# Spreading token scalars over a graph by VectorE and transfers instead of a matmul, with softmax, weight sums and seams moved, in a four-layer graph network

## The chip, the core and the metric

The kernel runs on one core of a Trainium2 chip. The core has five engines with a queue each, which work in order and meet through semaphores: TensorE (PE; its weight loads are listed as PEld), VectorE (DVE), ScalarE (ACT), GpSimd (POOL) and SyncE (SP), which here only issues transfers. The metric is the device time of one execution in microseconds (us), the median of several runs. All data are fp32.

## The reference

The input x has 128 graphs of 64 nodes with 512 features. Each layer adds to x what it computes from h = relu(layernorm(x)):

```python
# layer 0 (att over the 64 nodes i of a graph; mask is all ones)
agg = einsum('bij,bjd->bid', adj, h @ Wk)
w   = inv_scale * mask * einsum('bid,bid->bi', h @ Wq, agg)
x   = x + softmax(w, axis=1)[:, :, None] * (h @ Wv)
# layer 1
weight = adj * exp(einsum('bqd,bkd->bqk', query, keyt))
x   = x + (weight / weight.sum(2)) @ value
# layer 2: 8 heads, scores * (adj + adj), softmax, context, output product
# layer 3
sj = (h @ Wv + bv) @ aw[:512];  si = (h @ Wv + bv) @ aw[512:]
e  = leaky_relu(sj[:, None, :] + si[:, :, None] + ab, 0.2)
tr = adj * exp(e) / (sum + 1e-12)
x  = x + relu(h @ Wk0 + tr @ h @ Wk1 + tr @ tr @ h @ Wk2 + biases)
```

Two places need a scalar per token on every token of its graph: the softmax of layer 0 (the minimum and the sum of 64 values w) and the sums sj + si of layer 3.

## The kernel before

Tokens are worked in 32 blocks of 256 (four graphs, two tiles of 128 partitions, TT = 2, N = 64). Every 512x512 product of a block is a Strassen-like `Product`: seven products of quarters, whose operand sums S1 to S4 POOL makes (`sums`, L270 to L274) and whose parts are put together from two PSUM tiles `ab` and `dc` taken from a pool of four. `first` and `second` do the early matmuls and then keep copies: `keep_ab` copies on ACT (p1, L335) and adds on DVE (u2, L336), `keep_dc` copies on ACT (p5, L344 or L348). `late` does the rest on top of them, and `store` (L358 to L362), `store_T` (L366 to L382) or `add_to` write the result with ACT, DVE and POOL. Only when those have read a PSUM tile may a later product take it. `side_by_side` runs two products next to each other, with slots between their parts in which other work is issued (`between`).

`norm` (L185 to L217) takes the statistics on DVE (L185, L186, ve L188, mv L189), rstd and nmr on POOL (L191, L193), h on ACT (L200). ACT's queue writes h to DRAM in two pieces, SP's queue reads it back in four as `part`, and DVE turns it in 32x32 squares into the feature-major hT (L243).

Layers 0 and 1 are interleaved in steps (two blocks of layer 0, then two of layer 1, four steps a period); layer 2 is a loop over 32 blocks; layer 3 is a generator `layer3_step`: the head makes y2 and y1 (L306), the tail y0, the denominators (L966), po (L449), y (L977), then the dots hu (L915) of block b+2. Its end, two neighbour sums later, is tz on ACT (L1013), POOL (L1015) and DVE (L1016), issued from the head of the next step.

The program does not fix the order of an engine's queue alone. A scheduler places instructions by its own costs, and `tc.issue_after(i)` keeps what is issued under it behind instruction i. `behind`, `read`, `kept_ab` and `tail` are such marks. `chore` is one of the weight sums that POOL makes ahead of a later layer (L104).

A token scalar is spread over its graph by a product: DVE multiplies an eye by the scalar, which gives a diagonal block `wd` (L616) or `di` (L920), and `graph_sums` multiplies it by the block-diagonal matrix of ones (L457). In layer 0, `layer0_end` then takes the minimum (L627), the two exps on ACT (L633, L638), the weights att (L640, L641) and updates x (L643). In layer 3, `layer3_in` adds sj (L934), the leaky relu (L940), exp on ACT (L941) and the adjacency (L943).

Of the kernel before, what the change touches and what calls it, by code (L numbers as in the profile page):

```python
# [13 lines left out]
P = 128  # L14
# [12 lines left out]
def kernel(ctx: ExitStack, tc: tile.TileContext, a: dict, out: bass.AP):  # L27
# [72 lines left out]
    def chore(n: int = 1):  # L100
        with tc.issue_after(behind[0].ins):
            for _ in range(min(n, len(chores))):
                w, (to, x, y) = chores.pop(0)
                nc.gpsimd.tensor_tensor(w[:, to], w[:, x], w[:, y], ALU.subtract)  # L104
# [63 lines left out]
    eye = const.tile([P, N], FP, tag="eye", name="eye")  # L168
    for g in range(2):
        h = slice(g * N, (g + 1) * N)  # L170
        nc.vector.memset(ones_bd[h, h], 1.0)
        nc.vector.tensor_copy(eye[h, :], ident[h, h])
# [4 lines left out]
    behind_norm, parted = {}, {}  # L177
    read, w2 = [None], []

    def norm(x, name: str, home):  # L180
# [13 lines left out]
        behind_norm.setdefault(0, (by_rows, summed_up))  # L194
        h = med.tile([P, TT, D], FP, tag="h", name=f"h_{name}", bufs=homes["h"])
# [60 lines left out]
    behind = [None]  # L256
# [21 lines left out]
    class Product:  # L278
# [77 lines left out]
        def store(self, y):  # L356
# [4 lines left out]
            nc.vector.tensor_tensor(y[:, 0, F:], self.c, self.u2, ALU.add)  # L361
            nc.gpsimd.tensor_tensor(y[:, 1, F:], self.u3, self.p5, ALU.add)  # L362

        def store_T(self, y, bias):
# [8 lines left out]
            for m in range(2):  # L373
                f = slice(m * P, (m + 1) * P)
                self.taken = nc.vector.scalar_tensor_tensor(
# [78 lines left out]
    def graph_sums(e, cols: int, name: str):  # L454

        ps = ps_sc.tile([P, cols], FP, tag="sc", name=f"sm_{name}")
        nc.tensor.matmul(ps, ones_bd, e, start=True, stop=True)  # L457
        return ps

    def reciprocals(e, name: str):  # L460

        den = graph_sums(e.rearrange("p t i -> p (t i)"), TT * N, name)
        r = small.tile([P, TT, N], FP, tag="r", name=f"r_{name}", bufs=2)
        nc.vector.reciprocal(r.rearrange("p t i -> p (t i)"), den)
        return r
# [56 lines left out]
    def setup1():  # L522
# [43 lines left out]
        folded(kt, qt, 1, m, lambda: layer0_end(0, *softmax))  # L566
# [29 lines left out]
    def layer0(b: int, x, adjT, hs, hT, aggs, between):  # L596
# [10 lines left out]
        w = small.tile([P, TT], FP, tag="w", name=f"w_{b}")  # L607
        for t in range(TT):
            nc.vector.scalar_tensor_tensor(
# [3 lines left out]


        wd = small.tile([P, TT, N], FP, tag="e", name=f"wd_{b}")
        tail[0] = nc.vector.tensor_tensor(  # L616
            wd,
            eye.unsqueeze(1).to_broadcast([P, TT, N]),
            w.unsqueeze(2).to_broadcast([P, TT, N]),
            ALU.mult,  # L620
        )
        return x, gv, w, wd

    def layer0_end(b: int, x, gv, w, wd):
        wrow = graph_sums(wd.rearrange("p t i -> p (t i)"), TT * N, f"w_{b}")
        mn = small.tile([P, TT], FP, tag="mx0", name=f"mn0_{b}")
        nc.vector.tensor_reduce(  # L627
            mn, wrow.rearrange("p (t i) -> p t i", t=TT), AX.X, ALU.min
        )
        nc.vector.tensor_tensor(w, w, mn, ALU.subtract)  # L630
        tot = small.tile([P, TT], FP, tag="tot", name=f"tot_{b}")
        for t in range(TT):
            nc.scalar.activation(  # L633
                wd[:, t, :], wrow[:, t * N : (t + 1) * N], AF.Exp, bias=mn[:, t : t + 1],
# [272 lines left out]
    def layer3_dots(b: int, x, adjT, hs):  # L907
# [3 lines left out]
        sij = small.tile([P, 2, TT], FP, tag="sij", name=f"sij_{b}")  # L911
        for s in range(2):
            for t in range(TT):
                hu = med.tile([P, D], FP, tag="agg", name=f"hu_{b}_{s}_{t}", bufs=2)
                nc.vector.scalar_tensor_tensor(  # L915
                    hu, hs[t], 1.0, us[s], ALU.mult, ALU.mult,
                    accum_out=sij[:, s, t : t + 1],
                )
        di = small.tile([P, TT, N], FP, tag="e", name=f"di_{b}")
        nc.vector.tensor_tensor(  # L920
            di,
            eye.unsqueeze(1).to_broadcast([P, TT, N]),
            sij[:, 1, :].unsqueeze(2).to_broadcast([P, TT, N]),
            ALU.mult,
        )
        sj = small.tile([P, TT], FP, tag="sj", name=f"sj_{b}")
        nc.vector.tensor_scalar(sj, sij[:, 0, :], c3, None, ALU.add)
        return x, adjT, hs, di, sj

    def layer3_in(b: int, x, adjT, hs, e, sj, made: dict):  # L930


        pi = graph_sums(e.rearrange("p t i -> p (t i)"), TT * N, f"i_{b}")
        nc.vector.tensor_tensor(  # L934
            e,
            pi.rearrange("p (t i) -> p t i", t=TT),
# [180 lines left out]
    begun = []  # L1117
# [7 lines left out]
    for i, (layer, b) in enumerate(steps):  # L1125
        if i == n_steps - 4:
            fetch2(0)
        if i == n_steps - 3:
            fetch2(1)
        if i == n_steps - 1:  # L1130
            fetch2(2)
        between = [[], [lambda: chore(3 if i < 4 else 1)], []]
        if i == 1:
            begun = []
# [5 lines left out]
        for n, end in begun:  # L1140
            between[n].append(end)
        begun = []
# [10 lines left out]
        elif i + 2 == n_steps:  # L1153
            between[0].append(lambda: prepare2(0))
        else:
            between[0].append(lambda: prepare2(1))
        if layer == 0:
            softmax = layer0(b, *loaded[b], *normed[i], aggs.pop(b, None), between)
            begun = [(0, lambda b=b, softmax=softmax: layer0_end(b, *softmax))]
# [18 lines left out]
    w3, made_in, ops3 = {}, {}, {}  # L1178
# [4 lines left out]
    def layer3_step(b: int, ahead: bool = True):  # L1183
# [4 lines left out]
        x, al = made_in.pop(b)  # L1188
        ops = ops3.pop(b)
        coming = normed3  # L1190

        def begin():
# [3 lines left out]
            if b + 2 < n_blk and ahead:  # L1196
                with tc.issue_after(kept_ab[0].ins):
                    normed3 = layer3_norm(b + 2)

        def attention():  # L1200
            if b + 1 < n_blk:
                layer3_in(b + 1, *coming, made_in)

        y = layer3_head(b, ops, [[begin], [ending.pop()], [attention]])
        yield
# [8 lines left out]
        if b + 2 < n_blk:  # L1214
            with tc.issue_after(kept.ins):
                if ahead:
                    normed3 = layer3_dots(b + 2, *normed3)
                    fetch3(b + 3)
                else:
                    fetch3(b + 2)  # L1220
# [154 lines left out]
```

## Time and profile before

| | |
|---|---|
| three runs | 2524.32, 2524.8, 2526.9 us (median 2524.8) |
| profiled execution | 2527.1 us, its span 2524.5 us |
| mean granted clock of TensorE | 0.996 |
| PE busy | 2487.0 us in 19488 instructions |
| DVE busy | 1822.0 us in 4590 |
| POOL busy | 1324.1 us in 1710 |
| ACT busy | 857.1 us in 2106 |
| h to DRAM, issue to landing | 2.1 us (median of 252) |
| part from DRAM | 2.8 us (median of 504) |
| adjT from DRAM, 64 KB in 256-byte pieces | 2.2 us (median of 64) |
| c from c_row, one row to 128 partitions | 6.4 us (one) |

A busy time is the time in which an engine has an instruction in work; PE's matmuls are pipelined, so their durations overlap and the distance between two starts is what counts. In an order of time, a start to the next start is therefore often shorter than the duration beside it. "Idle before" names what ended the wait of an engine. A granted clock of 0.50 means that TensorE ran at half speed in that stretch.

### The profile page before, as it was taken

How to read it: one execution, taken by the hardware profiler on the slowest of the kernel's cores; microseconds unless marked ns; L12 is line 12 of the kernel's file. 1: busy time of each engine (PE TensorE's matmuls, PEld its weight loads, DVE VectorE, ACT ScalarE, POOL GpSimd, SP SyncE). 2: the span in 40 equal slices, each digit the busy share in tenths (PEclk: the TensorE clock that was granted, in tenths of full speed). 3: DMA queues.
4: the chain of work that ended last, by engine and by line, in shares of the span. 5: the costliest groups of instructions: out<-in, count | busy, mean ns of one | idle time of the engine just before them, and what ended most of it. 6: DMA issues, size and time to landing. Idle time of an engine off the chain costs nothing.

```text
span 2524.5 us, 52284 instructions
## 1 busy us (share of the span) xinstructions
PE 2487.0 (99%) x19488; PEld 2124.1 (84%) x19488; DVE 1822.0 (72%) x4590; ACT 857.1 (34%) x2106; POOL 1324.1 (52%) x1710
## 2 busy tenths in 40 slices
PE   9899999999999999999999999999989999999999
PEld 5788888888888888999999999999867777777776
DVE  5577777777777786667667667667568777777775
ACT  3333433333334332333333333333223333333332
POOL 2444343444433445666656556556465555555554
PEclk9999999999999999999999999999999999999999
DMA  7344343333343354443343343344433333333320
GB/s 180 94 127 124 111 127 114 119 107 116 113 126 112 122 156 138 128 133 108 122 132 115 123 131 115 122 136 134 139 112 104 104 103 107 105 106 106 103 77 34
DMA packets 305190, 295.50 MB, mean 117 GB/s; under 512 B 56870, under 2 KB 211494, under 8 KB 304936
## 3 DMA queue, kind: packets, MB, share of 16 engines
q1 hardware_dynamic: 258856, 208.26, 29.2%
q10 hardware_dynamic: 46080, 83.91, 9.1%
q8 instruction: 153, 2.51, 0.4%
q14 instruction: 101, 0.83, 0.1%
HBM read 158.91 MB, written 133.18 MB: 116 GB/s over the span
## 4 chain that ended last, share of the span: by engine, by line
PE 57%; DVE 2%; DMA 1%; POOL 1%; issue 1%; SPq 0%; ACT 0%; POOLq 0%; ACTq 0%; DVEq 0%
PE ab_y L306 13%; PE dc_y L306 9%; PE ab_v L306 4%; PE ab_q L299 4%; PE ab_k L299 4%; PE ab_o L306 4%; PE dc_q L299 3%; PE dc_k L299 3%; PE dc_v L306 3%; PE dc_o L306 3%; PE po L449 2%; PE pc L825 1%; PE s L750 1%; DVE hu L915 1%; DMA x<-x 0%
## 5 line engine op out<-in xcount | busy, mean ns | idle before, releaser
L200 ACT ACTIVATE h<-x,nmr,rstd 128x512 f32<-128x512 f32 x256 | 194.8, 806 | 207.6 <-POOL nmr L193 202.1
L270 POOL TENSOR_TENSOR S<-hT 128x256 f32<-128x256 f32 x128 | 97.8, 764 | 243.9 <-DVE hT L243 231.1
L306 PE MATMUL ab_y<-L_Wk,hT 128*128 128x256 f32 x768 | 204.9, 389 | 7.9 <-DVE u_y L336 6.7
L306 PE MATMUL ab_v<-L_Wv,hT 128*128 128x256 f32 x768 | 201.0, 384 | 3.7 <-DVE u_v L336 3.0
L306 PEld LDWEIGHTS ab_y<-L_Wk,hT 128*128 128x128 f32 x768 | 138.7, 190 | 74.9 <-DVE u_y L336 30.7
L191 POOL TENSOR_TENSOR rstd<-ve,neghalf 128x2 f32<-128x2 f32 x128 | 90.5, 707 | 209.2 <-DVE mv L189 190.7
L306 PE MATMUL dc_v<-L_Wv,S 128*128 128x256 f32 x768 | 198.0, 380 | 0.7 <-ACT p_v L344 0.7
L306 PE MATMUL ab_y<-L_Wk,S 128*128 128x256 f32 x768 | 198.0, 380 | 0.0
L306 PE MATMUL ab_v<-L_Wv,S 128*128 128x256 f32 x768 | 197.1, 379 | 0.0
L306 PE MATMUL dc_y<-L_Wk,S 128*128 128x256 f32 x768 | 193.5, 380 | 0.1
L243 DVE STREAM_TRANSPOSE hT<-part 128x512 f32<-128x512 f32 x252 | 174.4, 698 | 8.6 <-DMA part<-h_rows 5.9
L306 PEld LDWEIGHTS dc_y<-L_Wk,S 128*128 128x128 f32 x768 | 146.0, 191 | 21.3 <-issue 0.8
L306 PEld LDWEIGHTS ab_y<-L_Wk,S 128*128 128x128 f32 x768 | 146.5, 191 | 20.1
L185 DVE BATCH_NORM_STATS2 stats<-x 128x6 f32<-128x512 f32 x256 | 162.8, 677 | 0.0
L306 PEld LDWEIGHTS ab_v<-L_Wv,S 128*128 128x128 f32 x768 | 145.9, 190 | 19.8
L306 PEld LDWEIGHTS dc_v<-L_Wv,S 128*128 128x128 f32 x768 | 143.8, 191 | 20.0 <-ACT p_v L344 0.9
L306 PEld LDWEIGHTS ab_v<-L_Wv,hT 128*128 128x128 f32 x768 | 138.2, 190 | 21.9 <-DVE u_v L336 4.0
L915 DVE SCALAR_TENSOR_TENSOR hu<-h,us 128x512 f32<-128x512 f32 x128 | 139.4, 1139 | 1.9 <-POOL bs L894 1.4
L1015 POOL TENSOR_TENSOR tz<-tz,y 128x512 f32<-128x512 f32 x62 | 90.4, 1458 | 95.4 <-ACT tz L1013 95.3
L336 DVE TENSOR_TENSOR u_v<-ab_v,p_v 128x256 f32<-128x256 f32 x96 | 40.4, 421 | 126.4 <-ACT p_v L335 125.9
L1016 DVE SCALAR_TENSOR_TENSOR x<-tz,x 128x512 f32<-128x512 f32 x62 | 42.9, 692 | 112.3 <-POOL tz L1015 112.3
L272 POOL TENSOR_TENSOR S<-hT,S 128x256 f32<-128x256 f32 x128 | 113.0, 883 | 0.0
(257 smaller groups left out, 6181.7 us busy)
## 6 DMA issues: line engine op xcount, KB each, us to landing
x<-x SPq DMA_DIRECT2D x128, 512.0 KB, 3.8
h_rows<-h ACTq DMA_DIRECT2D x252, 256.0 KB, 2.1
part<-h_rows SPq DMA_DIRECT2D x504, 128.0 KB, 2.8
x<-in_x_dram SPq DMA_DIRECT2D x32, 512.0 KB, 3.7
e_rows<-et ACTq DMA_DIRECT2D x64, 256.0 KB, 3.0
pT<-e_rows SPq DMA_DIRECT2D x128, 128.0 KB, 3.1
out_dram<-x SPq DMA_DIRECT2D x31, 512.0 KB, 2.8
adjT<-in_adjT_dram SPq DMA_DIRECT2D x64, 64.0 KB, 2.2
```

The lines of the kernel that those rows point to most:

```text
L185: nc.vector.bn_stats(stats[:, t, :], x[:, t, :])
L191: nc.gpsimd.tensor_tensor(rstd, ve, neghalf, ALU.pow)
L200: nc.scalar.activation(hs[t], x[:, t, :], AF.Relu, bias=nmr[:, t : t + 1], scale=rstd[:, t : t + 1])
L243: nc.vector.transpose(hT[:, :, t * P : (t + 1) * P].rearrange("p k (g q) -> p g k q", q=Q), part[:, t * 4 : (t + 1) * 4].rearrange("p g (k ...
L270: nc.gpsimd.tensor_tensor(S1, A21, A22, ALU.add)
L272: nc.gpsimd.tensor_tensor(S4, A12, S2, ALU.subtract)
L299: nc.tensor.matmul(dst[:, m * P : (m + 1) * P], w[:, place, k, m * P : (m + 1) * P], left[:, k, :], start=key not in self.begun, stop=last ...
L306: nc.tensor.matmul(dst, left[:, k, :], w[:, place, k, :], start=key not in self.begun, stop=last and k == 1, skip_group_check=True,)
L449: nc.tensor.matmul(ps[t][half[g ^ t]], e[half[g], t, :], us[t][half[g]], start=True, stop=True)
L915: nc.vector.scalar_tensor_tensor(hu, hs[t], 1.0, us[s], ALU.mult, ALU.mult, accum_out=sij[:, s, t : t + 1],)
L1015: nc.gpsimd.tensor_tensor(tz[t], tz[t], y0[:, t, :], ALU.add)
L1016: nc.vector.scalar_tensor_tensor(x[:, t, :], tz[t], 0.0, x[:, t, :], ALU.max, ALU.add)
```

## The change

Token scalars no longer go through PE. They are written into the first two columns of a 128x32 tile that is zero elsewhere (`column_pair`, two of them in turn), DVE transposes its 32x32 squares into `lines`, SP writes the lines to a row in DRAM and reads it back twice, each time broadcast over the 64 partitions of a graph (`spread`). `graph_sums`, `eye`, `wd` and `di` as products are gone; 64 transposes, 128 row writes and 128 broadcast reads are added.

`layer0_end` of an even block (and of blocks 1 and 31) is issued in a new last slot of the next step, behind the DVE work of a store; that of the other odd blocks in the first slot of the step after the next, behind the norm's statistics. In layer 3, `layer3_in(b)` belongs to step b itself, norm(b+2) is placed behind the transfers of the last spread, and the load of x for b+3 behind the reads of h. POOL's weight sums are placed behind POOL's last store and behind nmr. At the seams the loads of layer 2 come earlier, its first norms behind the end of layer 0's step; the turn of e of block 31, the biases, loads, norms and dots of layer 3's first blocks are moved among the last three blocks of layer 2.

```diff
-    def chore(n: int = 1):
-        with tc.issue_after(behind[0].ins):
+    def chore(n: int = 1, also=()):
+        with ExitStack() as placed:
+            for i in (behind[0], *also):
+                placed.enter_context(tc.issue_after(i.ins))
...
-    def graph_sums(e, cols: int, name: str):
-
-        ps = ps_sc.tile([P, cols], FP, tag="sc", name=f"sm_{name}")
-        nc.tensor.matmul(ps, ones_bd, e, start=True, stop=True)
-        return ps
...
+    def spread(pair, name: str):
+
+        row = tc.dram_tile([TT, P], FP, name=f"{name}_row")
+        lines = small.tile([P, Q], FP, tag="lines", name=f"{name}_lines", bufs=2)
+        nc.vector.transpose(lines, pair)
+        for t in range(TT):
+            nc.sync.dma_start(
+                row[t : t + 1].rearrange("o (s q) -> (o s) q", q=Q), lines[t::Q]
+            )
+        to = small.tile([P, TT, N], FP, tag="e", name=name)
+        by_graph = row.rearrange("(o t) (g i) -> g o t i", o=1, g=2)
+        for g in range(2):
+            spread_out[0] = nc.sync.dma_start(
+                to[half[g]], by_graph[g].to_broadcast([N, TT, N])
+            )
+        return to
...
     def layer0_end(b: int, x, gv, w, wd):
-        wrow = graph_sums(wd.rearrange("p t i -> p (t i)"), TT * N, f"w_{b}")
...
-        nc.vector.tensor_reduce(
-            mn, wrow.rearrange("p (t i) -> p t i", t=TT), AX.X, ALU.min
-        )
+        nc.vector.tensor_reduce(mn, wd, AX.X, ALU.min)
...
-        between = [[], [lambda: chore(3 if i < 4 else 1)], []]
+        between = [[], [
+            lambda: chore(3 if i < 4 else 1, (stored[0], normalised[0]) if i else ())
+        ], [], []]
...
-            begun = [(0, lambda b=b, softmax=softmax: layer0_end(b, *softmax))]
+
+            late = b % 2 and 1 < b < n_blk - 1
+
+            def end0(b=b, softmax=softmax, late=late):
+                with tc.issue_after((counted[0] if late else stored[1]).ins):
+                    layer0_end(b, *softmax)
+
+            begun.setdefault(i + (2 if late else 1), []).append((0 if late else 2, end0))
...
             if b + 2 < n_blk and ahead:
-                with tc.issue_after(kept_ab[0].ins):
+                with tc.issue_after(kept_ab[0].ins), tc.issue_after(spread_out[0].ins):
                     normed3 = layer3_norm(b + 2)
 
         def attention():
-            if b + 1 < n_blk:
-                layer3_in(b + 1, *coming, made_in)
+            layer3_in(b, *dots3.pop(b), made_in)
...
                 if ahead:
-                    normed3 = layer3_dots(b + 2, *normed3)
-                    fetch3(b + 3)
+                    dots3[b + 2] = layer3_dots(b + 2, *normed3)
+                    with tc.issue_after(read[0].ins):
+                        fetch3(b + 3)
...
+        if b == n_blk - 2:
+            with tc.issue_after(read[0].ins):
+                fetch3(2)
+                fetch3(3)
+            with tc.issue_after(of_o.taken.ins):
+                pTs = layer2_turned(b + 1, es)
+            with tc.issue_after(read[0].ins):
+                bias3 = biases3()
```

## The prediction

> **What bounds the kernel now.** I read the page's header first, then the groups of TensorE (PE) by form, PE's waits, a table of stretches, and last the order of time of one layer-3 step.
>
> From the page:
>
> ```profile
> span 2524.5 us, 52284 instructions
> PE 2487.0 (99%) x19488; PEld 2124.1 (84%) x19488; DVE 1822.0 (72%) x4590; ACT 857.1 (34%) x2106; POOL 1324.1 (52%) x1710
> PE   9899999999999999999999999999989999999999
> ```
>
> PE is busy 99% of the span; only the second slice and the thirty-first show idle time. The groups that the change removes, from the groups by form (busy us, mean ns | idle before):
>
> ```profile
> L457 PE MATMUL sm_w<-wd,ones_bd 128*128 128x128 f32 x64 | 12.5, 277 | 4.5 <-DVE wd L616 4.5
> L457 PE MATMUL sm_i<-di,ones_bd 128*128 128x128 f32 x64 | 12.4, 275 | 0.0
> ```
>
> Those 277 ns overlap their neighbours. In the order of time sm_i starts at 2006.00 and the next matmul at 2006.22, so a pair takes 0.22 us of PE's row; 64 pairs are 14.1 us. PE's waits (total, times, longest):
>
> ```profile
> PE ab_y L306 <- DVE u_y L336: 6.7, 2, 6.5
> PE sm_w L457 <- DVE wd L616: 4.5, 2, 3.9
> PE ab_g L306 <- DVE u_g L336: 3.9, 2, 3.2
> PE pc L825 <- DMA pT<-e_rows: 2.8, 2, 1.7
> ```
>
> All are single events of a seam. The stretches say the same (us, then busy us of PE, PEld, DVE, ACT, POOL, granted clock, DMA share, GB/s):
>
> ```profile
> 60.00:100.00 40.00, 31.85 (x135) 24.57 (x136) 17.88 (x47) 12.00 (x31) 20.04 (x24) 0.91 0.45 126
> 580.00:640.00 60.00, 59.93 (x418) 51.34 (x417) 43.39 (x119) 22.86 (x60) 25.62 (x40) 1.00 0.39 119
> 1844.00:1904.00 60.00, 57.75 (x337) 45.35 (x338) 39.49 (x101) 17.71 (x39) 38.17 (x47) 0.96 0.37 109
> 2000.00:2060.00 60.00, 60.00 (x319) 47.25 (x319) 46.79 (x121) 19.48 (x40) 33.93 (x41) 1.00 0.32 103
> ```
>
> In the loops PE never waits: a gain there is only what leaves PE, and every new chain has to stay below PE's pace. So I followed the changed queue orders against these durations, from the order of time of one step (start, duration, engine, line):
>
> ```profile
> 2011.96 1.28 DVE L185 BATCH_NORM_STATS2 stats<-x 128x6 f32<-128x512 f32 x2
> ...
> 2014.82 1.52 ACT L200 ACTIVATE h<-x,nmr,rstd 128x512 f32<-128x512 f32 x2 [1.91 <-POOL nmr L193]
> 2015.67 1.03 ACTq L204 DMA_DIRECT2D h_rows<-h  x2
> ...
> 2018.55 0.91 DVE L915 SCALAR_TENSOR_TENSOR hu<-h,us 128x512 f32<-128x512 f32 x1
> ...
> 2022.78 0.22 DVE L927 TENSOR_SCALAR sj<-sij,c 128x2 f32<-128x2 f32 x1
> ...
> 2024.31 2.09 ACT L1013 ACTIVATE tz<-po,r 128x512 f32<-128x512 f32 x3 [0.59 <-PE po L449]
> ...
> 2026.37 0.69 DVE L1016 SCALAR_TENSOR_TENSOR x<-tz,x 128x512 f32<-128x512 f32 x1 [2.52 <-POOL tz L1015]
> ...
> 2028.83 0.42 DVE L359 TENSOR_TENSOR u_y<-ab_y,p_y 128x256 f32<-128x256 f32 x1
> ```
>
> The norm (L185 to h) runs in mid-step, long before the tail's end needs ACT for tz. L359 frees the PSUM tile that y0's first product takes next (PE starts it at 2029.71).
>
> **Layer 3, steps.** Removed: 0.22 us of PE, the product di (0.21 us to the next start) and eye. Added: one 128x32 transpose, two row writes and two broadcast reads on SP. Moved: norm(b+2) now stands on DVE straight behind hu, sj and the transpose, so its h stands on ACT ahead of the copy of dc (L344) and of tz, with its two DMA issues. ACT works its queue in order, so both wait for h. From the rows, beginning at hu's start 2018.55: four hu end at 2022.78; sj 0.13 (to the next start); the transpose is not in the trace: between sj's 0.13 and the 0.63 of a 128x512 L243, I take 0.15 since it is small: 2023.06. L185 twice 1.19, L186 twice 0.16, a u_y between them 0.33, L188 0.10, L189 0.16: 2025.00. POOL: rstd to nmr 0.78, nmr to h 0.22: h at 2026.01 instead of 2014.82. From h to the next ACT work, behind both DMA issues, 1.91 (565.70 to 567.61): the dc copy at 2027.92, where the trace has 2023.35. Then tz 0.27 later, L1015 0.76, L1016 1.30, L359 0.61, its end 0.42, PE 0.06: y0 begins at 2031.34.
>
> The cycle closes through y0: its start to po 3.68 (2008.81 to 2012.49), to L977 about 1.10 without the norm between, to hu 4.83: 9.61. With 12.79 from hu to the next y0 that is 22.4 us a step, against 20.90 now and 20.68 if PE still set the pace. That is +1.5 us. The transfers lie under it: transpose at 2023.06, second write issued 0.4 later, landing 2.1 as h_rows, second read 0.4 later, landing 2.2 as adjT, also in pieces of 256 bytes: L934 could start at 2028.3 and is needed by 2029.6, so there is 1.3 us of margin. Other rows bound it: c_row's write took 6.3 and c's broadcast 6.4, beside the weight loads of the start; I take the steady loops' rows. About 28 steps have this form: +42 us. Bounds: if hu took 0.83 each, as its first does here, the cycle is 21.2 (+9 in all); if the spread takes 1 us over its margin, +70.
>
> [...]
>
> **Layers 0 and 1, steps** (period of four steps 55.8 us, some 14 alike). Removed: two pairs, −0.44, and DVE's wd and eye. The softmax of an even block goes behind the next step's stores, that of an odd block to the first step after next, and what it delays is next in its queue. In the first layer-1 step, DVE has the two x updates (1.33), L361 (0.34), the statistics (1.19) and two transposes (1.23) before mv, and POOL has four S sums ahead of rstd; in the trace rstd stood before them (564.69, sums from 566.35). From 561.83: transposes done 566.3, the last three sums at 0.69 each 568.6, rstd and nmr 1.0: h at 569.6, not 565.70; p_v 1.91 behind it, u_v done 0.8 later, 572.3. PE wants it at 571.75 − 0.44: a wait of 1.0. In the second step everything runs 0.56 later (1.0 − 0.44): layer 1's x update ends 577.95 + 0.56 = 578.5, e·adj 0.2, statistics 1.2, aggregates and mv 0.5: 580.4; POOL 1.0: h at 581.4; behind h and its issues (1.91) stand the two exps 0.6 and ex: att at 584.3, x 1.4, u_g 0.4: 586.1. In between DVE does mn and two transposes under that cover. PE wants u_g at 583.78 + 0.56 + 0.43 (a pass of pa that now comes first) = 584.8: a wait of 1.3. Net +1.9 a period, 14 periods: +26. These queues are full and my errors add up: bounds −0.44 (everything still covered, −6) to +3.3 (S sums slowed to 1.17 as at 571 and no early pass, +46). I take the sums' unslowed rows, since hc comes after them.
>
> **Seams.** Start: the sm_w stall of 3.88 goes with its half-clock stretch, and POOL's weight sums leave the front of nmr (3.2): about −7 of some 12 lost; SP's queue behind the first spreads holds x loads back, up to +2. Layers 1 to 2: 3.5 us of waits, earlier fetches, −1 (0 to −3). Layers 2 to 3: the 6.51 wait at 1844 came from an ACT issue of e_rows that waited for DVE behind late hu's; the turn of block 31 moves ahead: −6.5, −1.7 for the clock, and some of the two pT waits, −10 in all (−6 to −13; a wait of si_of(0) ahead of u_q could put 2 back). Together −18.
>
> PE's clock: the trace grants 0.50 in 1818.6 to 1821.8 after waits of 1.68 and 1.08 us close together, yet single gaps of 1.3 to 1.7 elsewhere leave it at 1.00. The new waits are of this single size, so I charge nothing; a drop would cost about 1.7 us each. [...]
>
> **Sum.** The profiled execution took 2527.1 us (span 2524.5 and 2.6 around it): +42 +26 −18 −1 (the four periods and steps outside the loops' count) = 2576. The median is 2.3 lower than that execution: 2574.
>
> **Rivals.**
> Both loops wait (mine): 2574, own range 2545 to 2605. For it: the orders are fixed and ACT is served in order. Chance 0.54.
> One loop only: layer 3 alone 2527 + 42 − 6 − 18 − 2 = 2543; layers 0 and 1 alone 2527 + 26 − 6 − 18 − 2 = 2527 (0.05). Against it: the chains are independent of each other. 0.18, of which 0.03 within 0.2% (5 us, about what a measurement of this kernel can tell from none).
> Faster: PE keeps the pace everywhere. Place: layer 3 between hu and L359; it decides if that chain is 1.7 us shorter, which hu at 0.83 each (1.2) and an ACT that needn't wait for its DMA issues (0.4) nearly give. Price: −14.1 − 18 − 2.3 = 2493. Layer 0 and 1's covers must hold as well. 0.18.
> More: the spread ends last, or the clock halves at the waits: 28 x 1.0 or 1.7 on top, 2605 to 2660. 0.10.
>
> The range leaves out about half of the fastest case and most of the last: 2492 to 2610. Faster 0.18, same 0.03, slower 0.79.
>
> **What would show it.** After: PE's busy share near 96%, a layer-3 period of 22.4 with PE ab_y waiting for DVE L360 (L359 now) some 28 times at 1.5 to 1.8 us, h at the head's end; PE waiting for u_v and u_g in layer 1's steps; no sm rows; the 6.51 wait gone. If the layer-3 period is 20.7 and PE has no new wait, the chain of h through ACT was wrong; if L934 waits for the DMA, the spread was.

## The result and the profile after

The changed kernel takes 2635.79 us (median of 4 runs, 2631.8 to 2638.53) against 2525.72 of the kernel before on the same chip: a ratio of 1.0435, 95% interval 1.0417 to 1.0453. The prediction was 2574 with a range of 2492 to 2610. It was right that the change is slower and wrong in how much: the loss is 110 us, where 49 were forecast. One point of the description was not exact: the softmax of an even block stands in the third of the four slots, ahead of the second late part of the step, not in the last. The ratios below are against the kernel before, run beside each variant.

From the page of the kernel after:

```profile
span 2636.7 us, 52414 instructions
PE 2512.7 (95%) x19360; PEld 2117.1 (80%) x19360; DVE 1841.6 (70%) x4588; ACT 848.2 (32%) x2106; POOL 1306.0 (50%) x1712
PE   8999999999999999999999999999989888988898
PE 56%; DVE 22%; issue 6%; POOL 6%; ACT 4%; DMA 4%; ACTq 1%; SPq 1%; DVEq 0%; POOLq 0%
```

PE fell from 99% to 95% of a longer span, and the slices that lost are the last third, layer 3. The fourth row is the chain that ended last: DVE carries 22% of it. PE's waits (total, times, longest):

```profile
PE ab_y L307 <- DVE u_y L360: 52.6, 30, 2.6
PE dc_v L307 <- ACT p_v L345: 24.0, 16, 2.2
PE dc_y L307 <- DVE y L362: 11.8, 17, 0.7
PE ab_y L307 <- DVE u_y L337: 10.6, 28, 0.7
PE ab_g L300 <- DVE u_g L337: 4.7, 13, 1.2
```

Waits that come 13 to 30 times are waits of a loop, where before there were only single ones. The same stretches as before (us, busy us of PE, PEld, DVE, ACT, POOL, granted clock, DMA share, GB/s):

```profile
60.00:100.00 40.00, 36.76 (x170) 27.81 (x169) 24.25 (x67) 17.32 (x43) 23.46 (x30) 1.00 0.58 168
580.00:640.00 60.00, 58.31 (x399) 49.14 (x398) 41.45 (x119) 21.26 (x56) 22.21 (x36) 1.00 0.37 111
2000.00:2060.00 60.00, 54.45 (x280) 41.61 (x281) 46.89 (x108) 14.64 (x33) 32.05 (x38) 1.00 0.34 102
```

The start gained 4.9 us of PE in its 40; layers 0 and 1 lose 1.6 in 60, layer 3 loses 5.6 in 60.

To split the time, I took as marks PE's first pass in the first and in the last step of the scores `sc` of layer 1, the contexts `pc` of layer 2 and the denominators `den` of layer 3:

| stage, us | before | after | forecast of the difference | measured |
|---|---|---|---|---|
| start, to the first `sc` | 125.1 | 119.2 | −7 | −5.9 |
| layers 0 and 1 (period) | 833.8 (55.83) | 873.6 (58.73) | +26 (+1.9) | +39.7 (+2.9) |
| seam 1 to 2 | 38.6 | 38.6 | −1 | 0 |
| layer 2 to the first `den` | 862.3 | 851.7 | −10 | −10.6 |
| layer 3 (step) | 652.2 (20.90) | 740.9 (23.57) | +42 (+1.5) | +88.7 (+2.7) |

The seams are as forecast, −16.5 against −18. The forecast of the profiled execution, 2576, less the 2.6 around the span, was missed by 63 us; layer 3 holds 47 of them and layers 0 and 1 hold 14.

### The profile page after: what moved, and what is told of

Its sections match the earlier page's. It is cut to its first block, busy times and chain, and to the rows that moved or that the text cites. A ratio compares the mean times of both kernels' runs of the same rounds, so it can differ in the third digit from the quotient of the medians.

```text
span 2636.7 us, 52414 instructions
## 1 busy us (share of the span) xinstructions
PE 2512.7 (95%) x19360; PEld 2117.1 (80%) x19360; DVE 1841.6 (70%) x4588; ACT 848.2 (32%) x2106; POOL 1306.0 (50%) x1712
## 4 chain that ended last, share of the span: by engine, by line
PE 56%; DVE 22%; issue 6%; POOL 6%; ACT 4%; DMA 4%; ACTq 1%; SPq 1%; DVEq 0%; POOLq 0%
PE ab_v L307 9%; PE dc_v L307 6%; DVE hu L923 5%; PE ab_q L300 4%; PE ab_k L300 4%; PE ab_o L307 4%; PE ab_g L307 4%; PE dc_q L300 3%; PE dc_k L300 3%; PE dc_o L307 3%; DVE stats L185 3%; PE dc_y L307 3%; PE po L450 2%; PE dc_g L307 2%; DVE y L977 2%
## 5 line engine op out<-in xcount | busy, mean ns | idle before, releaser
L307 PE MATMUL ab_y<-L_Wk,hT 128*128 128x256 f32 x768 | 210.4, 397 | 63.4 <-DVE u_y L360 52.6
L307 PEld LDWEIGHTS ab_y<-L_Wk,hT 128*128 128x128 f32 x768 | 139.9, 192 | 143.8 <-DVE u_y L360 64.7
L307 PE MATMUL dc_v<-L_Wv,S 128*128 128x256 f32 x768 | 201.6, 382 | 24.0 <-ACT p_v L345 24.0
L307 PE MATMUL dc_y<-L_Wk,S 128*128 128x256 f32 x768 | 196.1, 384 | 12.9 <-DVE y L362 11.8
L307 PE MATMUL ab_v<-L_Wv,hT 128*128 128x256 f32 x768 | 201.3, 385 | 4.1 <-DVE u_v L337 1.7
L307 PE MATMUL ab_y<-L_Wk,S 128*128 128x256 f32 x768 | 200.4, 384 | 0.0
L307 PE MATMUL ab_v<-L_Wv,S 128*128 128x256 f32 x768 | 197.1, 379 | 0.0
L307 PEld LDWEIGHTS dc_v<-L_Wv,S 128*128 128x128 f32 x768 | 142.3, 190 | 44.9 <-ACT p_v L345 26.9
L307 PEld LDWEIGHTS dc_y<-L_Wk,S 128*128 128x128 f32 x768 | 145.5, 192 | 40.2 <-DVE y L362 18.6
L307 PEld LDWEIGHTS ab_y<-L_Wk,S 128*128 128x128 f32 x768 | 148.6, 193 | 20.7
L307 PEld LDWEIGHTS ab_v<-L_Wv,S 128*128 128x128 f32 x768 | 146.1, 190 | 19.6
L307 PEld LDWEIGHTS ab_v<-L_Wv,hT 128*128 128x128 f32 x768 | 139.4, 190 | 23.7 <-DVE u_v L337 3.3
L336 ACT COPY p_y<-ab_y 128x256 f32<-128x256 f32 x96 | 35.7, 372 | 340.3 <-PE ab_y L307 335.8
L1015 POOL TENSOR_TENSOR tz<-tz,y 128x512 f32<-128x512 f32 x62 | 88.2, 1423 | 100.9 <-ACT tz L1013 97.4
L363 POOL TENSOR_TENSOR v<-u_v,p_v 128x256 f32<-128x256 f32 x64 | 46.6, 729 | 127.6 <-DVE u_v L360 68.5
```

Source lines behind the costliest of these rows:

```text
L307: nc.tensor.matmul(dst, left[:, k, :], w[:, place, k, :], start=key not in self.begun, stop=last and k == 1, skip_group_check=True,)
L363: stored[0] = nc.gpsimd.tensor_tensor(y[:, 1, F:], self.u3, self.p5, ALU.add)
L1015: nc.gpsimd.tensor_tensor(tz[t], tz[t], y0[:, t, :], ALU.add)
```

## Experiments in layer 3

My theory was the order: norm(b+2) behind hu puts h ahead of tz on ACT, and so delays the release of y0's PSUM tiles. The rivals: the landing of the spread ends last, or the clock halves after the waits.

**e1_load_free** takes the mark off the load of x, which is what fixes the place of the norm; the transfers stay.

```diff
-                    with tc.issue_after(read[0].ins):
-                        fetch3(b + 3)
+                    fetch3(b + 3)
```

> The changed kernel with one edit: in layer 3 the load of x for block b+3 is no longer placed behind the reads of h. The scheduler then puts norm(b+2) into the middle of the step again (behind u_y of y0, ahead of L977), and h on ACT ahead of the step, not between the copies of dc; L934 stands behind the first L1016 and ahead of the second. Theory A (the norm's h on ACT ahead of the dc copy and tz makes the step): the layer-3 period falls from 23.6 to PE's own 20.7, the whole to about 2555 us. Theory B (the landing of the spread, ahead of L1016 and L360 on DVE, makes the step): the period stays at 23 or above, 2620 us or more. Both in turn (A first, then the landing 5.9 us after the transpose becomes the last): about 21.9, 2590 us.

Measured: 2580.59 us, ratio 1.0215 (1.02 to 1.023), layer 3 686.1 us, most steps 21.85. The norm is back in mid-step, and 55 of the 89 us went with it: the third case of the expectation, both in turn. What is left in PE's waits is one row:

```profile
PE ab_y L307 <- DVE u_y L360: 32.6, 30, 2.5
```

Here L934 stands between the two L1016, and DVE idles 59.9 us in all ahead of it for the spread's transfer. So with the order mended the landing is what ends last: about 1.2 us a step.

**e5_load_and_norm_free** also takes the spread's mark off the norm; by the scheduler's order L934 then falls behind both L1016 and the first L360.

```diff
-                with tc.issue_after(kept_ab[0].ins), tc.issue_after(spread_out[0].ins):
+                with tc.issue_after(kept_ab[0].ins):
...
-                    with tc.issue_after(read[0].ins):
-                        fetch3(b + 3)
+                    fetch3(b + 3)
```

> As e1, and norm(b+2) of layer 3 is no longer placed behind the spread. The scheduler keeps the norm in mid-step and puts L934 behind both L1016 and the first L360, so the landing of the spread is no longer ahead of what frees y0's PSUM tile. If the two causes are the norm's h on ACT and the landing ahead of L1016 and L360, both are gone here and PE sets the pace: layer-3 period 20.7, the whole near 2547 us. If something else of the spread costs (its 256 issues on SP, the transposes, DMA beside the loads), the period stays near the 21.85 of e1, about 2580 us.

Measured: 2542.36 us, ratio 1.0064 (1.0049 to 1.0079), layer 3 647.3 us, a step 20.68. That is PE's own pace: 0.22 below the step of before, the pair of sm_i that was removed.

```profile
2300.00:2360.00 60.00, 60.00 (x316) 47.19 (x315) 47.67 (x122) 19.40 (x40) 36.03 (x42) 1.00 0.32 104
```

So the transfers cost nothing where the first instruction that needs them stands late enough in DVE's queue. What is left against before is in layers 0 and 1.

**e2_l3_sums_on_pe** does the reverse: layer 3's scalars go through PE again, and the order stays as changed.

```diff
-        di = spread(pair, f"si_of_{b}")
+        di = small.tile([P, TT, N], FP, tag="e", name=f"di_{b}")
+        diagonal(di, pair[:, :TT])
...
+        pi = graph_sums(e.rearrange("p t i -> p (t i)"), TT * N, f"i_{b}")
```

> The changed kernel with layer 3's sums made on TensorE again (a diagonal block on DVE, 0.2 us more as two instructions, and the 0.22 us matmul); norm, loads and all other places as in the changed kernel, no spread transfers in layer 3. Theory A (h on ACT ahead of tz): the period stays near the chain of the prediction, 22.4 to 22.8, about 2600 us, without the steps at half clock. Theory B (the landing): the period falls to the 20.9 of before, about 2545 us.

Measured: 2636.02 us, ratio 1.0434 (1.0418 to 1.0449), a step 24.10. Without one transfer of a token scalar in layer 3 the time is that of the changed kernel, but the step missed the 22.4 to 22.8 that I expected of the order alone.

```profile
PE sm_i L459 <- ACT tz L1030: 40.2, 29, 1.4
PE ab_y L307 <- DVE u_y L337: 25.0, 28, 0.9
```

PE now waits for tz itself, the instruction that stands behind h on ACT. This is a wait of the product sm_i, which the changed kernel doesn't have. So e2 alone does not tell what the transfers cost; that is left to the next run.

**e9_in_behind_store** keeps the change and its order of the norm, but puts `layer3_in` (L934 to L943) behind the DVE work of a store, so that the landing can hold nothing up.

```diff
         def attention():
-            layer3_in(b, *dots3.pop(b), made_in)
+            with tc.issue_after(stored[1].ins):
+                layer3_in(b, *dots3.pop(b), made_in)
```

> The changed kernel with one edit in layer 3: layer3_in(b) is placed behind the store of y2 in its own head, so L934 and L940 stand behind both L1016 and the first L360 and their spread has landed a step earlier. The norm still follows the dots, with h on ACT ahead of the dc copy and tz. If the 1.2 us by which the step of the changed kernel exceeds the chain of the prediction (23.6 against 22.4) come from L934 waiting for the landing and L940 and L1016 then running beside POOL's L1015, the period is 22.4 to 22.6 here, the whole 2595 to 2605 us. If the chain itself was too short, the period stays at 23.6 and the whole above 2620.

Measured: 2619.43 us, ratio 1.0369 (1.0352 to 1.0387), layer 3 725.7 us, 23.56 in nearly every step.

```profile
PE ab_y L307 <- DVE u_y L360: 36.0, 29, 1.6
PE dc_y L307 <- DVE y L362: 19.5, 28, 0.7
```

This is the second case of the expectation: the chain of the prediction was too short by itself. With the landing out of the way the order makes +73.5 us (725.7 − 652.2) of layer 3's +88.7; landing and clock add 15.2 on top of it. The two overlap, so these are not shares that add up: in e1, with the order mended, the landing alone still cost 34 us (686.1 − 652.2). In the changed kernel 17 of the steps are of the form of e9.

## Experiments in layers 0 and 1

I split a period at the scores: the long part runs from the second layer-1 step's `sc` to the first one's (both layer-0 steps lie in it), the short part from there to the second's. Medians of the steady periods:

| us | long | short | period |
|---|---|---|---|
| before | 39.40 | 16.43 | 55.83 |
| after | 40.57 | 18.16 | 58.73 |
| e4_no_late | 40.57 | 20.35 | 60.9 |
| e7_h_first | 38.89 | 18.83 | 57.71 |
| e11_softmax_slot0 | 41.57 | 16.85 | 58.41 |
| e12_no_early_pa | 40.58 | 17.52 | 58.10 |
| e3_layer0_as_before | 39.90 | 16.43 | 56.32 |

**e3_layer0_as_before** puts layer 0's sums on PE and its softmax in its old place, ahead of the turn and of the norm; layer 3 and the seams stay changed.

```diff
-        return x, gv, w, spread(pair, f"w_of_{b}")
+        wd = small.tile([P, TT, N], FP, tag="e", name=f"wd_{b}")
+        tail[0] = diagonal(wd, w)
+        return x, gv, w, wd
...
-            begun.setdefault(i + (2 if late else 1), []).append((0 if late else 2, end0))
+            begun.setdefault(i + 1, []).insert(0, (0, end0))
```

> The changed kernel with layer 0 as before: sums of w on TensorE and the softmax in the first slot of the next step, ahead of the transposes; weight sums, loads, seams and layer 3 as in the changed kernel. Theory (the place of the softmax and the order it brings cost layers 0 and 1 their time): the four-step period goes from 58.73 back to 55.83, the whole to about 2595 us. Rival (the weight sums behind POOL's store and nmr, and the loads, cost it): the period stays at 57 or above, 2612 us or more.

Measured: 2613.81 us, ratio 1.0345 (1.0327 to 1.0362). The period is 56.32; 0.5 of it against before comes from a diagonal that this kernel makes by two instructions of 64 partitions, since e8, which has two, is at 56.34 and e10, the same with one, at 55.83. The whole missed the 2595 that I expected: the start goes back to 125.0, so its gain belongs to layer 0's spread, and layers 0 and 1 keep 12 us over before.

**e4_no_late** gives the odd blocks the place of the even ones.

```diff
-            late = b % 2 and 1 < b < n_blk - 1
+            late = False
```

> The changed kernel with the softmax of every block, odd ones too, in the slot ahead of the second late part of the next step. If the odd blocks' late softmax in the second layer-1 step costs most (exps and x update ahead of u_g, the early pass of pa): the four-step period falls by 1.5 or more, to 57.2 or less, about 2615 us. If the first layer-1 step costs most (x updates, transposes and S sums ahead of rstd, so h ahead of the copies of v): the period falls by less than 0.7, 2626 us or more.

Measured: 2647.73 us, ratio 1.0486 (1.047 to 1.0501), with the wait for p_v in both layer-1 steps:

```profile
PE dc_v L307 <- ACT p_v L345: 46.3, 27, 2.2
```

Neither case of the expectation came; the period rose. The short part grows by 2.19: the odd block's softmax now costs the wait for p_v in the second step as well. Of the change's two places the late one is the cheaper.

**e7_h_first** puts the norm ahead of the turn in the first layer-1 step, so that POOL's rstd stands before the four S sums.

```diff
-            between[0 if i else 2].append(lambda: turned(i + 1))
+            def turn_next():
+                if layer and not b % 2 and i + 2 < n_steps and counted[0]:
+                    with tc.issue_after(counted[0].ins):
+                        turned(i + 1)
+                else:
+                    turned(i + 1)
+
+            if layer and not b % 2 and i + 2 < n_steps:
+                between[0].append(lambda: prepare(i + 2))
+            between[0 if i else 2].append(turn_next)
...
-            between[0].append(lambda: prepare(i + 2))
+            if not (layer and not b % 2):
+                between[0].append(lambda: prepare(i + 2))
```

> The changed kernel with one order changed: in the first layer-1 step of a period the two transposes of the next step (and so their four sums on POOL) are placed behind mv, so that rstd and h of the norm come ahead of them. If the wait of dc_v for p_v (1.5 us, 16 times) is made by h coming late behind those sums, it goes and the period falls from 58.73 to 57.2, about 2613 us. If the x updates ahead of the statistics make it, the wait stays above 1 us and the period above 58.3, 2630 us or more.

Measured: 2614.99 us, ratio 1.0363 (1.0334 to 1.0393). The long part falls to 38.89, 0.51 below before, about the 0.44 of two removed pairs; so the place of the norm, behind the turn and the S sums, was the whole loss of the first step. But the short part grows by 0.67, with waits in other places:

```profile
PE dc_v L307 <- ACT p_v L345: 12.9, 12, 2.4
PE ab_v L307 <- DVE u_v L337: 12.4, 13, 1.2
```

**e11_softmax_slot0** keeps layer 0's spread but gives the softmax its old place, ahead of the turn.

```diff
-                with tc.issue_after((counted[0] if late else stored[1]).ins):
-                    layer0_end(b, *softmax)
+                layer0_end(b, *softmax)
...
-            begun.setdefault(i + (2 if late else 1), []).append((0 if late else 2, end0))
+            begun.setdefault(i + 1, []).insert(0, (0, end0))
```

> The changed kernel with the spread in layer 0 kept, but the softmax of every block in the first slot of the next step, as before. If the place of the softmax alone makes the cost of layers 0 and 1, the period goes to about 56. If the landing of the spread, 5.8 us behind the transpose, has to be waited for by the minimum on DVE with the stores and u's queued behind it, the period stays at 58 or above.

Measured: 2632.09 us, ratio 1.0424 (1.0407 to 1.0441). The short part is nearly mended (16.85), the long one is worse (41.57): 0.3 us a period better than the change and 2.1 worse than the sums on PE in that same place. The row that took over, and the minimum on DVE in e11 and in the changed kernel (busy us, mean ns of one, then idle before):

```profile
PE ab_v L307 <- DVE u_v L337: 16.0, 17, 1.1
```

```profile
L635 DVE TENSOR_REDUCE mn<-w_of 128x2 f32<-128x128 f32 x32 | 9.0, 281 | 42.6 <-DMA w_of<-w_of_row 42.6
L635 DVE TENSOR_REDUCE mn<-w_of 128x2 f32<-128x128 f32 x32 | 8.8, 277 | 0.0
```

In the old place DVE waits 17 times for the transfer, 2.5 us each; in the changed kernel's places never. So in these layers the spread cost at every place that was tried: at the old place the scalar has not landed, and at the later ones the softmax delays the norm. A place that costs nothing, as e5 has one in layer 3, was not found; that there is none is not shown.

**e12_no_early_pa** changes the order of PE alone: pa and po may only be issued behind the last late matmul (`last_mm`). The queues of ACT, POOL and SP stay as they were; on DVE three small instructions of the first steps change places.

```diff
-        for t, to, at in neighbour_sums(pa, am, hs):
+        with ExitStack() as placed:
+            if b > 2:
+                placed.enter_context(tc.issue_after(last_mm[0].ins))
+            parts = neighbour_sums(pa, am, hs)
+        for t, to, at in parts:
...
-        parts = neighbour_sums(po, e, [v[:, t, :] for t in range(TT)])
+        with tc.issue_after(last_mm[0].ins):
+            parts = neighbour_sums(po, e, [v[:, t, :] for t in range(TT)])
```

> The changed kernel with TensorE's order alone mended in layers 0 and 1: pa and po may only be issued behind the last of the late matmuls of the two products, so that no pass of pa stands alone between the first and the late matmuls of the second layer-1 step and pa and po are no longer interleaved. The queues of the other engines stay as they are in steady state. If the unexplained 1.2 us of that step is the split of pa (about 0.8 for the pass that stands alone, 0.4 for pa and po in turn): the period of layers 0 and 1 falls from 58.73 to 57.4 - 57.9, the stage from 873.6 to about 858, the whole to 2615 - 2625. Rival: DVE and ACT are what is late there, and TensorE merely fills its wait with pa: then the wait for u_g grows by what pa no longer fills, and the period stays at 58.3 - 58.8, the whole at 2628 - 2638.

Measured: 2623.45 us, ratio 1.0378 (1.0361 to 1.0396), period 58.10, the short part down by 0.64: the time expected of the split of pa, with a period between those expected of it and of the rival: both have a share. The order of time of the changed kernel shows what went (start, duration); the last row is the whole of pa in the kernel before:

```profile
598.10 1.03 PE L307 MATMUL dc_v<-L_Wv,hT 128*128 128x256 f32 x4
599.06 1.07 PE L450 MATMUL pa<-h,am 64*64 64x512 f32 x2
600.06 0.94 PE L300 MATMUL dc_g<-S,fold 128*128 128x128 f32 x6
601.26 1.16 PE L300 MATMUL ab_g<-hT,fold 128*128 128x128 f32 x8 [0.27 <-DVE u_g L337]
...
589.48 1.95 PE L449 MATMUL pa<-h,am 64*64 64x512 f32 x16
```

Two pa passes alone take 1.00 us to the next start; the sixteen of before take 1.77 together, 0.22 for two. There the passes start four at a time (the first four from 589.48 to 589.50), while the two alone start one behind the other, 0.48 apart. In e12 the wait that they had filled comes to light:

```profile
590.01 0.35 ACT L336 COPY p_g<-ab_g 128x256 f32<-128x256 f32 x1
590.26 0.62 ACT L349 ACTIVATE p_g<-dc_g,u 128x128 f32<-128x128 f32 x2
590.93 1.16 PE L300 MATMUL dc_g<-S,fold 128*128 128x128 f32 x8 [0.77 <-ACT p_g L349]
```

So of the second step's +1.73 us, 0.64 is PE's order. The 1.09 that e12 leaves I put down to the queue of ACT, where h and the two exps stand ahead of p_g: 0.77 of it is the wait in the last row (13 such waits, 10.4 us in all), and the rest is not shown by itself.

## Experiments on the seams, and a better version

**e6_seams_alone** has all sums on PE and the old places in layers 0 and 3; what is left of the change are the seams and the place of POOL's weight sums. Its diff is those of e2, e3 and e5 together; the spread is never called:

```diff
-        return x, gv, w, spread(pair, f"w_of_{b}")
...
-        di = spread(pair, f"si_of_{b}")
```

> The changed kernel with the sums of layers 0 and 3 on TensorE, the softmax of layer 0 and the norm and load of layer 3 placed as before: what is left of the change are the moved loads, norms and dots at the seams and the weight sums behind POOL's store and nmr. By the stages of the other runs: layer 2 and its seams 11 less, nothing at the start (its gain came with layer 0's part), layers 0 and 1 at 55.83 to 56.32 a period (0 to +7), layer 3 as before: 2515 to 2523 us. If the seams need the spread for their gain: 2526 us.

Measured: 2528.76 us, ratio 1.0009 (1.0 to 1.0019). That is above both cases of the expectation. Layer 2 and its end gain 11 us, as in the other variants (9 to 13). The start gains nothing without the spread (126.3), and layers 0 and 1 lose 12 at the period of 56.34, that of the diagonals in two pieces, so that the whole is level.

**e8_mixed** takes e5's layer 3; in layer 0 only blocks 0 and 1 use the spread, later blocks the sums on PE in the old place. POOL's weight sums keep the added marks for the first steps alone. **e10_mixed_one_diagonal** is e8 with the diagonal in one instruction.

```diff
-        return x, gv, w, spread(pair, f"w_of_{b}")
+        if early:
+            return x, gv, w, spread(pair, f"w_of_{b}")
+        wd = small.tile([P, TT, N], FP, tag="e", name=f"wd_{b}")
+        tail[0] = diagonal(wd, w)
+        return x, gv, w, wd
...
-            lambda: chore(3 if i < 4 else 1, (stored[0], normalised[0]) if i else ())
+            lambda: chore(3 if i < 4 else 1, (stored[0], normalised[0]) if 0 < i < 4 else ())
```

> The parts that the other runs leave: seams as changed, layer 3 as in e5 (spread, norm in mid-step, L934 behind L360), layer 0 with the spread in blocks 0 and 1 only and the sums on TensorE with the softmax in its old place from block 2 on, weight sums behind POOL's store and nmr in the first steps only. Start 6 less than before, layers 0 and 1 at 55.83, layers 2 and 3's seams 11 less, layer 3 at 20.7 (5 less): about 2504 us, faster than both. If layer 0's first two blocks push later ones or layer 3 stays at 21.85, 2530 us or more.

> As e8, with the diagonal block of layer 0 made by one DVE instruction as in the kernel before (eye kept, one column tile, lines in another pool slot). If the two half instructions made the 0.5 us by which e8's period (56.34) exceeds that of before, the period is 55.83 and the whole about 2503 us. If the place of the weight sums or the transposes makes it, the period stays at 56.3 and the whole at 2510.

Measured: e8 2509.98 us, ratio 0.9936 (0.9921 to 0.9951); e10 2505.01 us, ratio 0.9916 (0.9901 to 0.9931). e8 missed the 2504 expected by the 0.5 us a period of the diagonal in two pieces, which e10 takes away. So e10 beats both kernels: its periods are 55.83 in layers 0 and 1 and 20.68 in layer 3, and it keeps the gains of the start and of layer 2 (116.4 us to the first `sc`, and 848.9 from the first to the last `pc`, 858.4 before).

```profile
PE 2476.8 (99%) x19420; PEld 2113.7 (84%) x19420; DVE 1818.3 (73%) x4590; ACT 858.0 (34%) x2106; POOL 1327.2 (53%) x1711
```

## Why the prediction was right, and where it was wrong

**Layer 3: the chain was right, one term of the cycle was not.** The step that failed is "its start to po 3.68", the first piece of "y0 to hu 9.61": it took 4.75 us, because a second wait stands in it. One step of the changed kernel in order of time, of the form that 17 steps have; hu begins at 2275.36:

```profile
2279.75 0.20 DVE L471 STREAM_TRANSPOSE si_of_lines<-pair 128x32 f32<-128x32 f32 x1
...
2282.88 1.52 ACT L201 ACTIVATE h<-x,nmr,rstd 128x512 f32<-128x512 f32 x2 [3.11 <-POOL nmr L193]
...
2284.79 0.37 ACT L345 COPY p_y<-dc_y 128x256 f32<-128x256 f32 x1 [0.40 <-PE dc_y L307]
2285.06 2.10 ACT L1013 ACTIVATE tz<-po,r 128x512 f32<-128x512 f32 x3
...
2285.54 0.29 DVE L934 TENSOR_TENSOR si_of<-si_of,sj 128x128 f32<-128x128 f32 x1 [3.35 <-DMA si_of<-si_of_row]
2285.83 3.14 POOL L1015 TENSOR_TENSOR tz<-tz,y 128x512 f32<-128x512 f32 x2 [2.99 <-ACT tz L1013]
2285.86 1.38 DVE L940 SCALAR_TENSOR_TENSOR si_of<-si_of 128x128 f32<-128x128 f32 x1
...
2287.17 0.68 DVE L1016 SCALAR_TENSOR_TENSOR x<-tz,x 128x512 f32<-128x512 f32 x1
...
2287.77 0.41 DVE L360 TENSOR_TENSOR u_y<-ab_y,p_y 128x256 f32<-128x256 f32 x1
2288.24 1.13 PE L307 MATMUL ab_y<-L_Wk,hT 128*128 128x256 f32 x4 [1.23 <-DVE u_y L360]
...
2289.01 1.20 DVE L1016 SCALAR_TENSOR_TENSOR x<-tz,x 128x512 f32<-128x512 f32 x1 [0.83 <-POOL tz L1015]
...
2290.46 0.41 DVE L362 TENSOR_TENSOR y<-dc_y,u_y 128x256 f32<-128x256 f32 x1
...
2290.93 1.13 PE L307 MATMUL dc_y<-L_Wk,S 128*128 128x256 f32 x4 [0.69 <-DVE y L362]
```

From hu: h comes after 7.52 (forecast 7.46), the dc copy after 9.43 (9.37), L1015 after 10.47 (10.40), y0 after 12.88 (12.79). Each link of this half held to 0.1 us. The mis-sized term is the other half, "y0 to hu 9.61". Its first piece, "its start to po 3.68", is PE unstalled. But y0's dc tile is released by L362, which stands behind the second L1016, and that waits for the second L1015. I had followed the first of the two alone. Here y0 to po takes 4.75 (2288.24 to 2292.99), and y0 to the next hu 10.69 (2298.93). 12.88 + 10.69 = 23.57, the measured step. The second half is 1.08 over its term, 0.69 of it the wait for L362 and the rest what PE loses around its two waits. The second L1016 itself takes 1.20 us in the 17 steps that have this wait, and 0.69 in the kernel before. In each of them it begins just behind a POOL L363 (2289.01 against 2288.93 here); so about 0.5 us of the wait goes back to this stretch, which the sum didn't have either. Six late steps have neither this wait nor a lower clock, and there y0 to hu takes 9.73, close to the forecast's 9.61. The 1.08 with the 0.09 of the first half is 1.17 a step, over 27 distances 32 of the 47 us missing in layer 3; the other 15 are the next two points.

**The landing: margin 1.3 forecast, none found.** Transpose to L934 takes 5.79 here (forecast 5.2), up to 6.9 elsewhere. And what stands behind it is dearer than its row of before: L940, 0.32 us on the mean before, takes 1.24 to 1.41 beside POOL's L1015 and 0.30 in e1, where it is not beside it. So a step is on time only if L934 begins within about 10.4 us of hu, not 11.05. It did in 17 steps; in 11 it did not, and y0 began 14.1 to 14.3 us after hu. One of these:

```profile
2213.49 0.66 DVE L934 TENSOR_TENSOR si_of<-si_of,sj 128x128 f32<-128x128 f32 x1 [4.40 <-DMA si_of<-si_of_row]
2214.18 1.36 DVE L940 SCALAR_TENSOR_TENSOR si_of<-si_of 128x128 f32<-128x128 f32 x1
2215.47 0.68 DVE L1016 SCALAR_TENSOR_TENSOR x<-tz,x 128x512 f32<-128x512 f32 x1
```

As y0 comes later by then, its dc tile is free in time, so that a late landing alone costs only 0.2 to 0.5 us here. In the forecast's lower bound, hu at 0.83 each saves 0.9 us by its own rows (4.23 to 3.32), not 1.2: the cycle would be 21.5 and the loss 17 us, not 9.

**The clock: "I charge nothing" was wrong in five steps.** Five of the 11 late steps took 25.4 to 25.7 us, about 1.6 over their like, as the forecast had it for a drop (1.7). Six others with waits of 2.4 to 2.6 us took 23.8 to 24.0, so the length of a wait alone does not tell the two groups apart. The five records of a granted clock of 0.50 in these steps are 3.413 us long each and begin 35, 77, 15 and 14 times that apart. I laid the trace out in stretches of this length from them. Two such stretches with the ones behind them, first from the step above, whose wait is 2.63 us, then from one that kept its clock, with a wait of 2.64:

```profile
2212.65:2216.06 3.41, 1.25 (x6) 0.76 (x4) 2.54 (x3) 2.22 (x6) 2.53 (x2) 1.00 0.39 129
2216.06:2219.48 3.42, 2.94 (x7) 2.41 (x8) 2.97 (x9) 0.09 (x1) 1.83 (x2) 0.50 0.81 236
2502.78:2506.20 3.42, 1.50 (x7) 1.35 (x8) 3.42 (x8) 0.57 (x2) 1.88 (x2) 1.00 0.64 157
2506.20:2509.61 3.41, 3.41 (x28) 2.06 (x27) 1.73 (x8) 0.74 (x2) 2.10 (x3) 1.00 0.99 300
```

PE idles 2.16 us of the first stretch and 1.92 of the third. In the stretches ahead of the five drops PE idled for 2.04 to 2.53 us, and in no other stretch of this layer up to PE's last matmul for more than the third's 1.92. In the kernel before, laid out the same way from its own records, the six stretches that 0.50 follows have 2.32 to 3.41 us of idle PE, and all others from its first record of the clock on 1.58 at most. That is what these two traces show; a limit that holds in general is not shown. In e9, where the order alone makes waits of 1.24 us on the mean and 1.6 at most, the granted clock is 1.00 in 2300 to 2360 and 0.999 on the mean, against 0.997 here; so I put the drops down to the late landings.

The rival "the spread ends last, or the clock halves" has a price, 2605 to 2660, that holds the result, but this would have been luck: by e9 its mechanism adds 15 of 89 us. In this order of the norm e9 caps everything that comes of the landing at 15.2, and no run separates the size of the spread's pieces from its two round trips.

**Layers 0 and 1: both waits were there, a third term was not.** First step, forecast −0.44 + 1.0: measured +1.17, so the wait is 1.6. Order of time:

```profile
582.48 0.72 POOL L273 TENSOR_TENSOR S<-hT,S 128x256 f32<-128x256 f32 x1
...
583.16 0.69 POOL L191 TENSOR_TENSOR rstd<-ve,neghalf 128x2 f32<-128x2 f32 x1
...
584.16 1.52 ACT L201 ACTIVATE h<-x,nmr,rstd 128x512 f32<-128x512 f32 x2 [4.16 <-POOL nmr L193]
...
586.40 0.38 ACT L345 COPY p_v<-dc_v 128x256 f32<-128x256 f32 x1
...
586.83 0.70 PE L307 MATMUL dc_v<-L_Wv,S 128*128 128x256 f32 x2 [1.42 <-ACT p_v L345]
```

This is the forecast's path: rstd behind the S sums, h, both DMA issues, then ACT's copies. It ends at the copy of dc rather than at u_v, because PE's next matmul takes dc_v first; h to that matmul is 2.67, forecast 2.7 to u_v. h itself came about 0.45 later against PE than in my sum. Second step, forecast +1.3: what e12 leaves is 1.09, and "a pass of pa that now comes first", 0.43 in my sum as cover, is in truth a cost of 0.64, since it is split off and interleaved with po. 0.6 + 0.4 in a period by 14 is the missing 14 us.

**Seams** were right in place and size: no wait of 6.5 us at the end of layer 2, and no stall of sm_w in the start. The range failed because layer 3's upper bound was taken from the landing alone, and not from a second release in the same cycle.

## What to carry to other kernels

When a step is moved in a queue, close the cycle through every buffer that the next iteration takes, not only through the first: here two tiles are freed by two instructions of one engine, 2.7 us apart (L360 at 2287.77, L362 at 2290.46), and the second decided. Look where the first reader of a transfer that takes the place of a product stands in its queue: in layer 3 the same transfers cost 1.2 us a step ahead of work that others wait for (e1) and nothing behind it (e5), by the place of one instruction. Try the parts of a bundle by themselves: the pieces of this change kept apart give 0.8% where the whole loses 4.4%.

## What the runs showed of the hardware

In layer 3 of the changed kernel two instructions of DVE took longer in most places where they began just behind one of POOL. L940 takes 1.24 us and more where it begins 0.01 to 0.32 us behind POOL's L1015, and 0.30 in e1. L1016 takes 1.20 where it begins 0.07 to 0.08 behind L363, 0.68 where it begins 0.15 ahead of it, and 1.75 to 1.77 where it begins 0.04 to 0.08 behind the second L1015; the one that begins 0.01 behind it (1975.63) takes 0.68. In e9 the first L1016 begins 0.10 ahead of the second L1015, overlaps it for 0.6, and takes 0.69. Two 64-row passes between full ones took 1.00 us of PE's row (changed kernel, 599.06), and 0.22 in a row of sixteen (before, 589.48). After an idle time of over 0.1 us the first four passes of PE's L307 took 0.97 to the next start in 96 of 98 groups of the changed kernel at full clock, where four mostly take 0.86 in the stream.
